# Two small buffers for normalised tokens, one reader for each bank, and a changed product order in a two-half transformer block

## The chip, the cores and the metric

The kernel runs on one core of a Trainium2 chip. The metric is the device time of one execution in microseconds (us). Engines: PE (TensorE, matmuls), DVE (VectorE), ACT (ScalarE), POOL (GpSimd) and SP (SyncE, whose queue issues nearly all DMAs).

## The reference

```python
emb = silu(t) @ ada_w + ada_b                        # t: (2, 512), ada_w: (512, 3072)
shift_msa, scale_msa, gate_msa, shift_mlp, scale_mlp, gate_mlp = split(emb, 6)
norm = ln(x) * (1 + scale_msa) + shift_msa           # x: (2, 2048, 512)
h = gelu(norm @ ssm_w1 + ssm_b1)                     # 512 -> 512
x = x + gate_msa * (h @ ssm_w2 + ssm_b2)             # 512 -> 512
norm2 = ln(x) * (1 + scale_mlp) + shift_mlp
hf = gelu_tanh(norm2 @ ff_w1 + ff_b1)                # 512 -> 1024
out = x + gate_mlp * (hf @ ff_w2 + ff_b2)            # 1024 -> 512
```

All of it is in float32.

## The kernel before

The 4096 tokens are cut into 8 blocks of 512 (`NBLK`, `TB`); in memory a block is 128 partitions of C = 4 tokens. Every product is made by a scheme with seven smaller products, P1 to P7, in place of eight; its operands are quarters of a matrix and sums of quarters. `first` and `second` make the sums: s[0], s[1], s[2] and one changed quarter ("21" or "12"). P5 needs s[0], P6 s[1]. Of the weights, made by `first`, P7 is the changed "21" and P3 is s[2]; of the tokens, made by `second`, P3 is the raw quarter "22", P7 the changed "12" and P4 is s[2].

**The first half** goes by block. For each block `norm1(i)` loads x into one of five slots (`xs`, 8 KB a partition), takes the statistics on DVE, makes 1/sigma from them on POOL (`scales`), normalises the four tokens of a partition one by one on ACT (`normal`), and turns each on DVE (`turn`, 32x32 transposes) into one of two buffers (`blocks`). The turned block goes to `turned[i]` (two places of 8 KB, by the parity of i): for block 2 in 16 DMAs (`move`), for blocks 3 to 7 out to DRAM in four (`turned_out`) and in again in one. There ACT scales and shifts it in four steps (`modulate`), and `norm1_sums` makes the token sums. Then `ssm1(i)` makes the first product with gelu, `ssm2(i)` the second, added to x in its slot; the slot is written out (`x1_d`), and `norm2(i)` normalises and turns it for the second half, out to DRAM in four DMAs. In `norm1`, `normal` writes into `turned[i]`; in `norm2` it writes in place, into `xs[i]`.

Blocks 0 and 1 are turned by PE (`turn_rows_in`), and ACT or DVE scales and shifts them on the way out of PSUM (`turn_rows_out`). Block 0 goes in two halves of two tokens each: half 0 is turned between the two halves of the product that makes the scale (`modulation(1, 2)`), half 1 after it. For each half, rows k = 0, 1 share one PSUM bank and k = 2, 3 another; DVE takes even k, ACT odd.

PE's order is the order of the program: the block-0 head, `ssm1(0)`, `ssm2(0)`, two modulations, `ssm1(1)`, the gate rows, `ssm1(2)`, then for i = 1 to 7 `ssm2(i)`, `ssm1(i + 2)`. `ssm1(0)` takes its products in the order `FRESH`, the later ones in `CARRIED`; small pieces of PE work (`gate_rows_of(2, 1)`, the gate of `first_weight2`) stand between its products by `hooks`. Banks come in two sets that take turns by stage.

**The second half** takes pairs of blocks, four times `ff1(s)` and two `ff2`. Its weights (`weight_fw1`, `weight_fw2`) are prepared during the first half in the space of the modulation weights.

**Order on the other engines.** All work is recorded as operations (`Plan.add`) with estimated costs, and a planner (`Plan.order`) places them: it gives each operation the latest time at which it must be done for PE not to wait, simulates the engines, and writes the instructions out in the order of their planned starts. Each engine then runs its list in order. Dependencies are found by the cells that an operation reads and writes (`Plan.cells`; a PSUM bank is one cell). `plan.care` lengthens, for what is recorded while it is set, the planned latencies and DMA times; it is 0.15 for `norm1(2)`, and from `norm2(0)` to the end 0.3.

The tiles' names in the profile stand for regions: `turned` for both places of turned tokens, `ring`, `rows`, `far` and `fw` (`fw2_r`) for the regions with x slots, `hidden` and `near` for gelu's output and the second weights. In the blocks' sequence `fw` holds x of block 4, `rows` of 2, 3 and 7, `ring` of 1 and 6, `far` of 0 and 5. L292 is every matmul, L302 a transpose on PE, L254 every addition or multiplication of two tensors, L272 every activation, L281 every copy on ACT, L314 every DMA, L502 and L503 the statistics, L510 to L523 `scales`, L543 `turn`, L608 DVE's eviction of block 0's tokens.

Of the kernel before, what the change touches and what calls it, by code (L numbers as in the profile page):

```python
# [20 lines left out]
class Plan:  # L21
# [44 lines left out]
    def add(self, engs, fn, outs, ins, cost, lat, shared="", size=0, lead=0.0):  # L66
        op = Op()
        op.n, op.engs, op.fn, op.cost, op.lat, op.shared, op.size = len(self.ops), engs, fn, cost, lat, shared, size
        op.deps, op.succ, op.note, op.lead, op.care = set(), [], self.stage, lead, self.care
        op.after, op.done, op.sooner = None, None, 0.0  # L70
        for ap in ins:
            for c in self.cells(ap):
                if c in self.wrote:
                    op.deps.add(self.wrote[c])
                self.read.setdefault(c, []).append(op.n)
        for ap in outs:
            for c in self.cells(ap):
                if c in self.wrote:
                    op.deps.add(self.wrote[c])
                op.deps.update(self.read.pop(c, ()))  # L80
                self.wrote[c] = op.n
        op.deps.discard(op.n)
        self.ops.append(op)
        return op
# [112 lines left out]
def kernel(  # L197
# [20 lines left out]
    KD, KH = D // P, H // P  # L218
# [121 lines left out]
    def kb(t, at, n):  # L340
        return t[:, at * 256 : (at + n) * 256]

    def cut(t, form, **sizes):
        return t.rearrange(form, **sizes)
# [27 lines left out]
    w1_s = cut(kb(ring_r, 8, 6), "p (s k d) -> p s k d", s=3, k=2)  # L372
    w2_t = [cut(kb(near_r, at, 8), "p (k d) -> p k d", k=KD) for at in (0, 14)]
    w2_s = cut(kb(near_r, 8, 6), "p (s k d) -> p s k d", s=3, k=2)
    hA = [cut(kb(hidden_r, 8 * (i % 2), 8), "p (k t) -> p k t", k=KD) for i in range(NBLK)]
    hA_s = [cut(kb(hidden_r, 16 + 6 * (i % 2), 6), "p (s k t) -> p s k t", s=3, k=2) for i in range(NBLK)]
    blocks = [kb(far_r, 8 * n, 8) for n in range(2)]
# [88 lines left out]
    def gate_rows_of(g, bank):  # L466
        pa = rows_of(g, bank)
        tt("v", gate_rows[g], pa[:, :P], gate_b[g], ALU.add)
        to = gates_d[g].rearrange("b (n m q) -> m b n q", n=KD, q=G)
        for m in range(M):  # L470
            dma(to[m], cut(gate_rows[g][m * G : m * G + B, :], "p (n q) -> p n q", n=KD))
# [34 lines left out]
    def scales(t, mv, v="g", slots=slice(0, C)):  # L506
# [16 lines left out]
            small(v, lambda E: E.tensor_scalar(nmr, nmr, -1.0, None, ALU.mult), nmr, [nmr])  # L523
        return full[3], full[4]

    def normal(o, xt, c, rstd, nmr, e="a"):
        dst, src, b, s = o[:, c, :], xt[:, c, :], nmr[:, c : c + 1], rstd[:, c : c + 1]
        if e == "a":
            act(dst, src, AF.Identity, b, s)
        else:  # L530
            plan.add(
                "v",
                lambda E: E.tensor_scalar(dst, src, s, b, ALU.mult, ALU.add),
                [dst],
                [src, b, s],
                {"v": 560},
                {"v": 640},
            )

    def turn(bl, src, c):  # L540
        o = cut(bl, "p (m k c q) -> p k m c q", m=C, k=KD, c=C)[:, :, :, c, :]
        a = cut(src[:, c, :], "p (k m q) -> p k m q", k=KD, m=C)
        plan.add("v", lambda E: E.transpose(o, a), [o], [a], {"v": 636}, {"v": 705})  # L543

    def modulate(t, k, which, b):
# [5 lines left out]
    def next_blocks():  # L551
        turns[0] += 1
        return blocks[turns[0] % 2]
# [9 lines left out]
    def normed(src, dst, bl, queues="s"):  # L563
        t, mv = stats(src)
        rstd, nmr = scales(t, mv)
        for c in range(C):
            normal(dst, src, c, rstd, nmr)
            turn(bl, dst, c)
        return cut(bl, "p (m r) -> p m r", m=C)
# [7 lines left out]
    def turned_out(to, bl):  # L577
        for a in range(C):
            dma(to[:, a].rearrange("(m q) r -> q m r", m=C), bl[a * G : (a + 1) * G])

    def norm1(i):
        plan.stage = f"norm1 {i}"
        load_x(i)
        bl = normed(xs[i], turned[i], next_blocks())
        if i in turned1_d:
            turned_out(turned1_d[i], bl)
            dma(turned[i], turned1_d[i])
        else:
            move(turned[i], bl)
        for k in range(KD):  # L590
            modulate(turned[i], k, 0, i // PER_B)
        return norm1_sums(i)

    def turn_rows_in(xn, k, to, slots=range(C), ends=(True, True)):
        for c in slots:
            at = (c - slots[0]) * P
            turn_by_pe(to[:, at : at + P], xn[:, c, k * P : (k + 1) * P], ident, c == slots[0] and ends[0], c == slots[-1] and ends[1])

    def turn_rows_out(i, k, to, e, slots=range(C)):
        n = len(slots)  # L600
        o = turned[i][:, :, k * P : (k + 1) * P].rearrange("p a (c q) -> p a c q", c=C)[:, :, slots[0] : slots[0] + n]
        a = cut(to, "p (c a q) -> p a c q", c=n, a=C)
        shift, scale = mods[0][:, k, :1], mods[1][:, k, :1]
        if e == "v":
            cost = 128.0 * n / 0.96 + 70
            plan.add(
                "v",
                lambda E: E.tensor_scalar(o, a, scale, shift, ALU.mult, ALU.add),  # L608
                [o],
                [a, scale, shift],  # L610
                {"v": cost},
                {"v": cost + 90},
            )
        else:
            act(o, a, AF.Identity, shift, scale)
# [14 lines left out]

    def norm2(i):
        plan.stage = f"norm2 {i}"
        turned_out(turned_d[i], normed(xs[i], xs[i], next_blocks()))

# [18 lines left out]

    PLAIN = ("P1", "P2", "P6", "P5", "P7", "P3", "P4")

    FRESH = ("P1", "P2", "P5", "P6", "P7", "P3", "P4")

    def between(hooks, p, stage):  # L660
        if p in hooks:
# [450 lines left out]
        for c in (2 * h, 2 * h + 1):  # L1112
            normal(xn, xs[0], c, rstd, nmr, "va"[c % 2])

    def turn_in(h, bank, k0):
        for k in (k0, k0 + 1):
            turn_rows_in(xn, k, banks[bank][:, k % 2 * W : (k % 2 + 1) * W], range(2 * h, 2 * h + 2), (k == k0, k > k0))

    def turn_out(h, on):
        for k in range(KD):  # L1120
            to = banks[on[k // 2]][:, k % 2 * W : (k % 2 + 1) * W]
            turn_rows_out(0, k, to, "va"[k % 2], range(2 * h, 2 * h + 2))

    normed_half(0)
    plan.add("v", lambda E: E.tensor_copy(cols_t[:, :ROWS], banks[1][:, :ROWS]), [cols_t[:, :ROWS]], [banks[1][:, :ROWS]], {"v": 130}, {"v": 200})
# [10 lines left out]
    pick = cut(ident, "p (m q) -> p m q", q=G)[:, :, :1].to_broadcast([P, M, P])  # L1136
    plan.add("v", lambda E: E.tensor_copy(picks, pick), [picks], [ident], {"v": 560}, {"v": 640})
    modulation(0, 1)
    modulation(1, 2, lambda: (turn_in(0, 0, 0), turn_in(0, 3, 2)))
    turn_out(0, (0, 3))  # L1140
    normed_half(1)
    w1q = {"11": w1_t[:, :2, : D // 2], "12": w1_t[:, 2:, : D // 2], "21": w1_t[:, :2, D // 2 :], "22": w1_t[:, 2:, D // 2 :]}
    turn_in(1, 4, 0)
    turn_in(1, 6, 2)
    turn_out(1, (4, 6))
    w1_ops = first(w1q, thirds(w1_s), "g")
    tok = {0: norm1_sums(0)}
    load_gate_b(2)
# [15 lines left out]
        gated[0] = weight2(0, 2)  # L1164

    plan.anchor = len(plan.ops)
    hid = {0: ssm1(0, tok[0], w1_ops, {"P6": lambda: gate_rows_of(2, 1), "P3": first_weight2}, FRESH)}
    w2_ops = gated[0]
    load_ada(3)
    load_ada(4)  # L1170
    load_gate_b(5)
    plan.care = 0.15
    tok[2] = norm1(2)
    plan.care = 0.0
    ssm2(0, hid[0], w2_ops, PLAIN, {"P2": turn_first, "P5": turn_second})
# [3 lines left out]
    load_ada(5)  # L1179
    modulation(4, 2)  # L1180
    hid[1] = ssm1(1, tok[1], w1_ops)
    tok[3] = norm1(3)
    gate_rows_of(5, 1)
    hid[2] = ssm1(2, tok[2], w1_ops)
# [72 lines left out]
```

## Time and profile before

| | us |
|---|---|
| median of 3 runs | 575.43 |
| lowest and highest | 575.0 and 576.33 |
| the profiled execution | 576.46 |
| its span | 574.7 |
| busy: PE, DVE, POOL, ACT | 564.4, 460.9, 322.7, 240.6 |

The profile is of one execution; its times count from the start of the span. The TensorE clock was granted in full throughout. A float32 matmul leaves two records in the trace, so that a product of four matmuls is 8 records. At the end of a row, in brackets, stands how long the engine had been idle and who released it.

### The profile page before, as it was taken

The page shows a single profiled execution, that of the slowest core. Times are in us where ns is not written, and L with a number is a line of the kernel's source. Part 1 is how long each engine was busy: PE and PEld are TensorE (multiplying, and loading weights), DVE is VectorE, ACT ScalarE, POOL GpSimd, SP SyncE. Part 2 cuts the span into 40 slices and gives each one's busy share as a digit, 9 for nine tenths or more (in the row PEclk, how much of TensorE's full clock was granted, in tenths as well). Part 3 has the DMA queues.
Part 4 walks back from the last instruction along what each step waited for, and adds up shares of the span by engine and source line. Part 5 has one row for each costly group of instructions (what it writes and reads, how often), then busy time and mean ns, then how long its engine had stood idle before and what let it go on. Part 6 is the DMA issues. An engine that isn't in the chain of part 4 may idle for free.

```text
span 574.7 us, 9495 instructions
## 1 busy us (share of the span) xinstructions
PE 564.4 (98%) x3301; PEld 503.4 (88%) x3301; DVE 460.9 (80%) x875; ACT 240.6 (42%) x417; POOL 322.7 (56%) x410
## 2 busy tenths in 40 slices
PE   7999999999998999999999999999999999999997
PEld 4788888888887888888999888999888999888997
DVE  5587757769877888889886789888889996789846
ACT  3463955656585624656002366002265112335010
POOL 2794347989853689954800435802896643436620
PEclk9999999999999999999999999999999999999999
DMA  8953798889998976884225644137855053520022
GB/s 316 398 204 79 216 306 299 272 332 278 347 273 288 326 254 224 280 283 166 74 74 170 236 170 165 55 112 254 294 173 188 1 146 119 195 91 1 2 74 73
DMA packets 49659, 112.20 MB, mean 195 GB/s; under 512 B 5152, under 2 KB 9164, under 8 KB 48076
## 3 DMA queue, kind: packets, MB, share of 16 engines
q1 hardware_dynamic: 48848, 111.05, 58.1%
q8 instruction: 26, 0.43, 0.3%
q10 hardware_dynamic: 764, 0.55, 0.3%
q14 instruction: 21, 0.17, 0.1%
HBM read 73.69 MB, written 36.84 MB: 192 GB/s over the span
## 4 chain that ended last, share of the span: by engine, by line
PE 87%; DMA 6%; ACT 2%; DVE 1%; POOL 1%; issue 1%; SPq 1%; DVEq 0%; ACTq 0%; POOLq 0%
PE bank L292 87%; DMA turned<-turned 3%; DMA fw<-in_L_cond_ada_w_dram 1%; DMA ring<-in_x_dram 1%; ACT turned L272 1%; SPq L314 1%; ACT hidden L272 1%; ACT fw L272 0%; DVE hidden L254 0%; POOL ring L254 0%; DVE marks L502 0%; PE bank L302 0%; POOL near L254 0%; POOL turned L254 0%; DVE turned L608 0%
## 5 line engine op out<-in xcount | busy, mean ns | idle before, releaser
L292 PE MATMUL bank<-turned,ring 128*128 128x256 f32 x896 | 205.8, 380 | 3.2 <-ACT turned L272 1.7
L292 PEld LDWEIGHTS bank<-turned,ring 128*128 128x128 f32 x896 | 168.9, 190 | 29.0 <-ACT turned L272 2.9
L254 DVE TENSOR_TENSOR hidden<-bank,hidden 128x512 f32<-128x512 f32 (+2 forms) x171 | 125.8, 757 | 40.0 <-PE bank L292 34.4
L254 DVE TENSOR_TENSOR rows<-bank,rows 128x256 f32<-128x256 f32 (+3 forms) x234 | 99.2, 457 | 30.0 <-PE bank L292 23.4
L292 PE MATMUL bank<-near,hidden 128*128 128x256 f32 x448 | 98.4, 380 | 0.2 <-POOL near L254 0.2
L292 PEld LDWEIGHTS bank<-near,hidden 128*128 128x128 f32 x448 | 84.9, 190 | 12.1 <-POOL near L254 0.5
L292 PE MATMUL bank<-ring 128*128 128x256 f32 x336 | 82.2, 381 | 0.0
L292 PE MATMUL bank<-fw,hidden 128*128 128x128 f32 (+1 forms) x512 | 80.1, 301 | 0.0
L281 ACT COPY bank<-bank 128x512 f32<-128x512 f32 (+2 forms) x66 | 31.7, 480 | 109.5 <-PE bank L292 109.1
L292 PEld LDWEIGHTS bank<-fw,hidden 128*128 128x128 f32 x512 | 72.9, 191 | 3.9
L292 PEld LDWEIGHTS bank<-ring 128*128 128x128 f32 x336 | 63.2, 190 | 10.6 <-POOL hidden L254 1.1
L292 PE MATMUL bank<-fw,far 128*128 128x128 f32 (+2 forms) x624 | 66.0, 286 | 0.2 <-DMA fw<-in_L_cond_ada_w_dram 0.2
L254 POOL TENSOR_TENSOR fw<-fw 128x256 f32<-128x256 f32 (+1 forms) x59 | 53.2, 921 | 18.8 <-DMA fw_parts<-fw 8.4
L292 PEld LDWEIGHTS bank<-fw,far 128*128 128x128 f32 (+1 forms) x624 | 59.8, 166 | 3.2 <-issue 0.8
L292 PE MATMUL bank<-fw,near 128*128 128x128 f32 (+1 forms) x432 | 59.5, 291 | 0.0
L254 POOL TENSOR_TENSOR turned<-turned 128x512 f32<-128x512 f32 (+1 forms) x43 | 48.1, 1134 | 14.9 <-ACT turned L272 8.0
L272 ACT ACTIVATE hidden<-hidden,cols 128x512 f32<-128x512 f32 (+1 forms) x66 | 43.3, 707 | 31.0 <-DVE hidden L254 30.8
L292 PEld LDWEIGHTS bank<-fw,near 128*128 128x128 f32 x432 | 54.9, 192 | 1.4
L254 POOL TENSOR_TENSOR hidden<-hidden 128x512 f32<-128x512 f32 (+1 forms) x34 | 42.5, 1257 | 23.7 <-ACT hidden L272 16.2
L272 ACT ACTIVATE turned<-turned,mod,mod 128x512 f32<-128x512 f32 x56 | 41.9, 804 | 19.1 <-DMA turned<-turned 18.7
L254 POOL TENSOR_TENSOR ring<-turned,ring 128x256 f32<-128x256 f32 x40 | 29.2, 735 | 26.4 <-PE bank L292 15.1
L254 POOL TENSOR_TENSOR ring<-turned 128x256 f32<-128x256 f32 x14 | 10.2, 726 | 47.0 <-PE bank L292 43.8
(104 smaller groups left out, 560.2 us busy)
## 6 DMA issues: line engine op xcount, KB each, us to landing
ring<-fw_parts SPq DMA_DIRECT2D x28, 512.0 KB, 6.0
turned<-far SPq DMA_DIRECT2D x52, 256.0 KB, 4.6
ring<-fw_parts SPq DMA_DIRECT2D x28, 384.0 KB, 3.0
turned<-turned SPq DMA_DIRECT2D x32, 256.0 KB, 4.8
rows<-x SPq DMA_DIRECT2D x32, 256.0 KB, 4.9
out_dram<-rows SPq DMA_DIRECT2D x29, 256.0 KB, 2.9
fw<-in_L_cond_ff_w_dram SPq DMA_DIRECT2D x12, 512.0 KB, 4.8
fw_parts<-fw SPq DMA_DIRECT2D x21, 256.0 KB, 3.3
```

What stands on the lines that cost most here:

```text
L254: lambda E: E.tensor_tensor(o, a, b, f),
L272: lambda E: E.activation(o, a, func, bias=bias, scale=scale),
L281: plan.add("a", lambda E: E.copy(o, a), [o], [a], {"a": cost}, {"a": cost + 60})
L292: lambda E: E.matmul(o, lhsT, rhs, start=start, stop=stop, skip_group_check=True, **kw),
L314: plan.add(q, lambda E: E.dma_start(out=o, in_=a), outs, ins, {q: plan.ISSUE}, {q: lat}, size=size, lead=lead)
```

## The change

- `passing`, two buffers of 2 KB a partition in space that was free (in `near` and `hidden`): `normal` writes tokens c = 0 and 2 into the first, 1 and 3 into the second, and `turn` reads them there; for `norm1(2)` to `norm1(7)` and `norm2(1)` to `norm2(7)`. For these blocks `turned[i]` and `xs[i]` are not written by `normal` any more.
- Block 0's turned tokens: each bank has one reader. Half 0: k = 0 in bank 3 and k = 2, 3 in bank 0 for DVE, k = 1 in bank 6 for ACT. Half 1: banks 1, 7 and 4, all for ACT. So DVE makes three evictions and ACT five, where each made four.
- `FRESH`: P3 moves ahead of P7. (P5 was third before.) The gate rows go behind P5, where they were behind P6; `first_weight2` goes behind P7, where it was behind P3 (the sixth product in either order).
- The planner orders readers of one PSUM bank on different engines one after the other, as dependencies of its own.
- `plan.care`: 0 in place of 0.15 for `norm1(2)`; 0.45 in place of 0.3 from `norm1(3)` on.

By the planner the order on DVE, ACT, POOL and SP changes in many places up to the second half; the instructions themselves stay nearly the same in number (DVE has 6 more, POOL 7 fewer, some sums having moved between them, ACT 1 more). PE's instructions are the same, in an order that differs in the head alone.

```diff
@@ Plan.add
+                if len(c) == 1:
+                    op.deps.update(n for n in self.read.get(c, ()) if self.ops[n].engs != engs)
...
+    passing = (kb(near_r, 24, 2), kb(hidden_r, 30, 2))
...
+    def slot(t, c):
+        return t[c % 2] if isinstance(t, tuple) else t[:, c, :]
@@ normal
-        dst, src, b, s = o[:, c, :], xt[:, c, :], nmr[:, c : c + 1], rstd[:, c : c + 1]
+        dst, src, b, s = slot(o, c), xt[:, c, :], nmr[:, c : c + 1], rstd[:, c : c + 1]
@@ turn
-        a = cut(src[:, c, :], "p (k m q) -> p k m q", k=KD, m=C)
+        a = cut(slot(src, c), "p (k m q) -> p k m q", k=KD, m=C)
@@ norm1
-        bl = normed(xs[i], turned[i], next_blocks())
+        bl = normed(xs[i], passing, next_blocks())
@@ norm2
-        turned_out(turned_d[i], normed(xs[i], xs[i], next_blocks()))
+        turned_out(turned_d[i], normed(xs[i], passing if i else xs[i], next_blocks()))
...
-    FRESH = ("P1", "P2", "P5", "P6", "P7", "P3", "P4")
+    FRESH = ("P1", "P2", "P5", "P6", "P3", "P7", "P4")
...
-    def turn_in(h, bank, k0):
-        for k in (k0, k0 + 1):
-            turn_rows_in(xn, k, banks[bank][:, k % 2 * W : (k % 2 + 1) * W], range(2 * h, 2 * h + 2), (k == k0, k > k0))
-
-    def turn_out(h, on):
+    ROOM = (((3, 0), (6, 0), (0, 0), (0, 1)), ((1, 0), (7, 0), (4, 0), (4, 1)))
+
+    def room(h, k):
+        bank, part = ROOM[h][k]
+        return banks[bank][:, part * W : (part + 1) * W]
+
+    def turn_in(h):
         for k in range(KD):
-            to = banks[on[k // 2]][:, k % 2 * W : (k % 2 + 1) * W]
-            turn_rows_out(0, k, to, "va"[k % 2], range(2 * h, 2 * h + 2))
+            turn_rows_in(xn, k, room(h, k), range(2 * h, 2 * h + 2), (k != 3, k != 2))
+
+    def turn_out(h):
+        for k in range(KD):
+            turn_rows_out(0, k, room(h, k), ("vavv", "aaaa")[h][k], range(2 * h, 2 * h + 2))
...
-    hid = {0: ssm1(0, tok[0], w1_ops, {"P6": lambda: gate_rows_of(2, 1), "P3": first_weight2}, FRESH)}
+    hid = {0: ssm1(0, tok[0], w1_ops, {"P5": lambda: gate_rows_of(2, 1), "P7": first_weight2}, FRESH)}
...
-    plan.care = 0.15
+    plan.care = 0.0
     tok[2] = norm1(2)
...
     hid[1] = ssm1(1, tok[1], w1_ops)
+    plan.care = 0.45
     tok[3] = norm1(3)
```

More of the change, by code (lines that the diff above doesn't have):

```diff
@@ L1138 @@
     modulation(0, 1)
-    modulation(1, 2, lambda: (turn_in(0, 0, 0), turn_in(0, 3, 2)))
-    turn_out(0, (0, 3))
+    modulation(1, 2, lambda: turn_in(0))
+    turn_out(0)
     normed_half(1)
     w1q = {"11": w1_t[:, :2, : D // 2], "12": w1_t[:, 2:, : D // 2], "21": w1_t[:, :2, D // 2 :], "22": w1_t[:, 2:, D // 2 :]}
-    turn_in(1, 4, 0)
-    turn_in(1, 6, 2)
-    turn_out(1, (4, 6))
+    turn_in(1)
+    turn_out(1)
     w1_ops = first(w1q, thirds(w1_s), "g")
```

## The prediction

> **What bounds the kernel now.** I read the parts of the page first, then busy time by stage, then TensorE's waits, then the timeline around each wait. The first part of the page shows one engine at the limit:
>
> ```profile
> PE 564.4 (98%) x3301; PEld 503.4 (88%) x3301; DVE 460.9 (80%) x875; ACT 240.6 (42%) x417; POOL 322.7 (56%) x410
> ```
>
> PE is busy for 564.4 of 574.7 us. The change alters neither the number nor the shape of any matmul; only in the head does it move some. So it can win only PE's idle time, and lose only by making more of it. Busy time by stage says where that is (after the length, each engine's busy us):
>
> ```profile
> 45.00:60.00 15.00, 15.00 (x135) 12.83 (x128) 9.85 (x26) 6.55 (x12) 4.89 (x16) 1.00 0.46 113
> ...
> 108.00:157.00 49.00, 48.62 (x226) 42.52 (x225) 37.83 (x76) 28.74 (x50) 45.06 (x66) 1.00 0.92 314
> 157.00:183.00 26.00, 24.28 (x113) 21.05 (x113) 21.80 (x41) 15.87 (x28) 11.17 (x19) 1.00 0.91 289
> ...
> 219.00:574.00 355.00, 351.54 (x2164) 322.23 (x2162) 296.02 (x550) 115.19 (x202) 175.86 (x185) 1.00 0.44 147
> ```
>
> From 219 on, the second half of the network, nearly all is PE: 351.54 of 355 us, and what is missing is mostly the last additions and the write. Between 45 and 60 PE never rests, between 108 and 157 it misses 0.38 us and between 157 and 183 1.72 us. TensorE's waits name the places:
>
> ```profile
> PE bank L292 <- ACT turned L272: 1.7, 1, 1.7
> ...
> PE bank L292 <- POOL turned L254: 0.9, 1, 0.9
> PE bank L292 <- DVE hidden L254: 0.4, 1, 0.4
> PE bank L292 <- POOL near L254: 0.2, 1, 0.2
> ```
>
> The 0.9 is in block 0's first product, the 0.4 in `ssm1(4)`, the 1.7 ahead of `ssm1(7)`; the 0.2 is in `ssm2(0)`. Little more than these can be won after the first 14 us, where nothing that the change touches binds.
>
> **The head (bank rooms, P3 ahead of P7).** The timeline of the head:
>
> ```profile
> 13.38 0.99 DVE L608 TENSOR_SCALAR turned<-bank,mod,mod 128x256 f32<-128x256 f32 x2
> ...
> 13.98 5.67 PE L292 MATMUL bank<-turned,ring 128*128 128x256 f32 x24 [0.21 <-DVE turned L608]
> 14.02 1.48 ACT L272 ACTIVATE turned<-bank,mod,mod 128x256 f32<-128x256 f32 x3 [2.01 <-DVE turned L608]
> ...
> 14.65 1.27 POOL L254 TENSOR_TENSOR ring<-ring 128x512 f32<-128x512 f32 x1 [4.57 <-DMA ring<-in_L_cond_ssm_w_dram]
> ...
> 16.10 0.56 ACT L272 ACTIVATE turned<-bank,mod,mod 128x256 f32<-128x256 f32 x1 [0.61 <-DVE turned L608]
> ...
> 16.70 0.69 DVE L254 TENSOR_TENSOR turned<-turned 128x512 f32<-128x512 f32 x1 [0.63 <-ACT turned L272]
> 17.23 0.33 SPq L314 DMA_DIRECT2D rows<-in_x_dram  x1
> 17.53 1.27 POOL L254 TENSOR_TENSOR ring<-ring 128x512 f32<-128x512 f32 x1 [1.61 <-DVE turned L254]
> ...
> 18.76 1.72 POOL L254 TENSOR_TENSOR turned<-turned 128x512 f32<-128x512 f32 x1
> ...
> 20.53 2.00 PE L292 MATMUL bank<-turned,ring 128*128 128x256 f32 x8 [0.88 <-POOL turned L254]
> ...
> 23.55 3.69 PE L292 MATMUL bank<-turned,ring 128*128 128x256 f32 x16
> ...
> 27.08 1.05 PE L292 MATMUL bank<-hidden,fw 128*128 128x128 f32 x8
> ```
>
> The eight evictions of block 0's turned tokens share banks between DVE and ACT, and each reader waits for the other (2.01 and 0.61 us on ACT), so the last ends at 16.66. Only then come DVE's sum s0 (16.70), POOL's weight sum behind it (17.53), POOL's token sum s1 (18.76, 1.72 long), and at 20.53 P6, which needs both. PE had finished P1, P2 and P5, 24 records from 13.98. Two products, 16 records, take 3.53 from the start at 23.55 to the next start at 27.08, 0.221 a record; 24 of these end at 19.28. So 20.53 - 19.28 = 1.25 us are lost.
>
> After the change the banks have one reader each, three evictions on DVE and five on ACT. An eviction takes 0.99 / 2 = 0.50, so from 13.38 DVE ends at 14.9 and ACT at 15.9. s0 needs only two early ones on ACT beside DVE's first: it can start at 14.95 and P5, at 17.5, has it. POOL's weight sum then follows its first one from about 15.9 on, and s1 ends near 18.5. The gate rows (formerly after P6; 23.55 - 20.53 less P6's 8 records is 1.25) now stand between P5 and P6, so P6 is due only at 20.5; their weights had landed by 17.2, when the row load that reuses that queue slot was issued. Cover for s1 is 2.0 us. The sum of q12 goes from DVE to POOL, and P3, which reads raw tokens, stands ahead of P7, which needs it: POOL's six sums in a row, at 1.27 each from 14.65, end at 22.3, and P7 is due at 20.5 + 2 x 1.77 = 24.0. The whole 1.25 goes: **-1.25**. Bounds: 0 if another sum is late by as much, and -1.4 if the waits inside P1 go too. I take -1.25 because each successor keeps over a microsecond of cover.
>
> [...]
>
> **Block 2's tokens (passing buffers, care 0).** With PE 1.25 earlier, what is due next? `ssm1(2)` at 59.39:
>
> ```profile
> 40.87 0.69 DVE L254 TENSOR_TENSOR far<-bank,far 128x512 f32<-128x512 f32 x1 [0.65 <-PE bank L292]
> ...
> 42.05 2.83 DVE L543 STREAM_TRANSPOSE far<-turned 128x512 f32<-128x512 f32 x4 [0.48 <-ACT turned L272]
> ```
>
> ```profile
> 44.95 10.94 SPq L314 DMA_DIRECT2D turned<-far  x16
> ...
> 46.26 1.26 DVE L502 BATCH_NORM_STATS2 marks<-rows 128x6 f32<-128x512 f32 x2
> ...
> 57.98 2.93 ACT L272 ACTIVATE turned<-turned,mod,mod 128x512 f32<-128x512 f32 x4 [0.35 <-issue]
> ...
> 59.39 2.86 PE L292 MATMUL bank<-turned,ring 128*128 128x256 f32 x12
> ```
>
> Four normalisations, four transposes, 16 moves on SP's queue (10.94), then ACT's four modulations from 57.98, 0.73 apart. P1 reads the first two; they end at about 58.8 and 59.5, for matmuls at 59.39 and 59.83. The margin is 0.3 to 0.6 us. The program's order of the changed kernel moves this chain back against PE: DVE's four transposes stand behind four statistics of block 3 and the addition that starts at 40.87. That addition is released by PE, so it comes at 39.6; with 0.69, two statistics (1.26 in the row at 46.26) and an aggregate the first transpose starts at about 41.7. The two small buffers now bind: normalisation 2 can start only when transpose 0 has ended (42.4), and so on through 0.8 and 0.7 us: transpose 3 ends at 44.6, against 42.05 + 2.83 = 44.88. The moves start only 0.3 earlier where PE comes 1.25 earlier. First matmul: ready 58.5, due 58.1, 0.4 lost; second: ready 59.2, due 58.9, 0.25 lost. **+0.65**. Bounds: 0, if the transposes come a microsecond sooner; +1.5, if block 3's tokens are awaited in front of them. The nearest rows are these.
>
> **Blocks 3 to 7 (passing buffers, care 0.45).** Two stalls remain:
>
> ```profile
> 95.76 12.25 PE L292 MATMUL bank<-near,hidden 128*128 128x256 f32 x56
> ...
> 107.84 10.52 PE L292 MATMUL bank<-turned,ring 128*128 128x256 f32 x48
> 107.95 0.41 SPq L314 DMA_DIRECT2D ring<-in_x_dram  x1
> ...
> 115.93 1.29 DVE L502 BATCH_NORM_STATS2 marks<-ring 128x6 f32<-128x512 f32 x2 [1.84 <-DMA ring<-in_x_dram]
> ...
> 117.93 0.67 DVE L254 TENSOR_TENSOR hidden<-bank,hidden 128x512 f32<-128x512 f32 x1
> ...
> 118.75 1.53 PE L292 MATMUL bank<-turned,ring 128*128 128x256 f32 x6 [0.39 <-DVE hidden L254]
> ```
>
> A product pair sequence of 56 records takes 107.84 - 95.76 = 12.08, 0.216 a record; 48 end at 118.19, and PE goes on at 118.75: 0.56 lost. DVE's addition at 117.93, which empties PE's bank, was behind statistics that waited for the load of x, issued at 107.95 and landed at 115.9. In the changed order all statistics of that time stand at the end of `ssm2(2)`'s additions, that is before 108, and x's slot is given back by ACT's normalisation and no longer by the in-place copy's transpose. The load is issued earlier on SP, right behind block 4's tokens. **-0.56**; bounds 0 and -0.56.
>
> ```profile
> 159.28 1.52 ACT L272 ACTIVATE turned<-rows,marks 128x512 f32<-128x512 f32 x2
> ...
> 162.16 6.62 SPq L314 DMA_DIRECT2D turned<-far  x8
> ...
> 168.89 3.88 SPq L314 DMA_DIRECT2D turned<-turned  x5
> 168.90 12.25 PE L292 MATMUL bank<-near,hidden 128*128 128x256 f32 x56
> ...
> 179.18 5.75 ACT L272 ACTIVATE turned<-turned,mod,mod 128x512 f32<-128x512 f32 x8 [7.78 <-DMA turned<-turned]
> ...
> 182.87 7.51 PE L292 MATMUL bank<-turned,ring 128*128 128x256 f32 x32 [1.72 <-ACT turned L272]
> ```
>
> ```profile
> 171.86 7.22 DMA turned<-turned
> ```
>
> `ssm1(7)` should follow 168.90 + 12.08 = 180.98 and starts at 182.87: 1.89 lost, to ACT's modulations, which waited for a load issued at 171.86. It took 7.22 us, behind four loads for the second half (the row at 168.89 holds all five). Block 7 was normalised at 159.28 into the place where it was to be loaded. In the changed order this load stands ahead of those four, two fw2 loads and one weight write before it, and ACT's modulations stand at the beginning of `ssm2(5)`, some 10 us before they are due. **-1.89**; bounds 0 (queue held by the fw2 loads, which wait for POOL) and -1.89.
>
> The new waits of the passing buffers lie on ACT: in each of 13 normalised blocks the third and fourth normalisation wait for a transpose, with ACT's next evictions queued behind them. Back to back two normalisations take 1.52 (159.28) and a transpose 0.7, so where DVE is prompt the wait is nothing. I put it at 0 where DVE is free; below nothing is excluded, since ACT does no less. The new dependencies between bank readers exist in the planner alone; they issue nothing.
>
> **Sum.** -1.25 + 0.65 - 0.56 - 1.89 = -3.05. The profiled execution took 576.46 (span 574.7), 1.03 above the median of 575.43; so changed, it would take 573.4, and the median 572.4.
>
> **Rivals.**
>
> Slower: ACT stuck behind the passing buffers. DVE is busy for 37.83 of the 49 us from 108 to 157, so a transpose can find one or two additions or statistics of 0.7 ahead of it; ACT stands meanwhile, and the copy of P1's sum behind it has only P5's 1.73 us of cover, less its own 0.57. Some eight of the 13 blocks have such a copy, or an eviction, close behind a waiting normalisation. It decides from 1.2 us of backlog on; 0.7 over at eight places is +5.6, and the time 575.43 - 3.05 + 5.6 = 578.0. Against it: the order is planned with these buffers, and most of the normalisations stand right behind a copy, not ahead. Chance 0.16.
>
> Block 7's load stays late: SP is one queue, in front of the load stand transfers that wait for POOL. Then -1.89 is missing: 574.3. For it: SP's issues of five loads took 3.88 us here. Against: 10 us of slack. Chance 0.15.
>
> POOL binds in the head. A DVE sum beside POOL's stretched it here to 1.72 from 1.27; if that happened four times and each cost a DVE sum's 0.7, POOL would be ready at 22.3 + 4 x 0.7 = 25.1 for P7 at 24.0, and 1.1 us would be lost: 573.5. [...] Chance 0.05.
>
> The change does not do what its title says: P5 stood third before already. What moves is P3 ahead of P7, which is worked out above; no separate time.
>
> **How the numbers follow.** The forecast has 0.64, the rivals 0.16, 0.15 and 0.05. The forecast's own range is 571.2 (no stall at block 2, all else gone: -3.7, and half a microsecond for the gap in `ssm2(0)`) to 573.9 (block 2 at +1.5 and the 0.56 kept). To hold 8 in 10 I go from 571.0 to 576.6, which takes in the late load and the start of the slower rival. About 0.2% (1.15 us) is what a measurement of this kernel can tell: faster lies below 574.3, slower above 576.6. The forecast and the head's rival are faster (0.69), of the late load about a third: 0.74; the rest of it is the same, 0.10; slower 0.16.
>
> **What would show it.** In the changed trace: P6 within 0.2 us of the end of the gate rows, no PE idle between 14 and 26; a wait of `ssm1(2)` for ACT's modulations of 0.4 to 0.7; none at `ssm1(4)` and `ssm1(7)`, with ACT's modulations of block 7 done by 175; PE's idle time between 14 and 219 below 1.5 us. I am wrong if ACT's evictions or seeds appear among PE's releasers with over a microsecond, or if the second half starts less than 1.5 us earlier than before.

## The result, and the profile after

| | before | changed |
|---|---|---|
| median of 6 runs, us | 575.97 | 573.32 |
| lowest and highest | 575.0 and 576.98 | 572.86 and 573.73 |
| the profiled execution | 576.46 | 572.99 |
| its span | 574.7 | 571.2 |

The ratio is 0.9953 with a 95% interval of 0.9939 to 0.9966: the changed kernel is faster by 2.65 us. The two profiled executions differ by 3.47. In the changed kernel's rows the lines have moved by 2 to 6: L294 is every matmul, L304 PE's transpose, L256 every addition of two tensors, L274 every activation, L316 every DMA, L505 the statistics, L549 `turn`, L614 DVE's eviction.

The first part of the page and busy time by stage (length, then the busy us of PE, PEld, DVE, ACT and POOL):

```profile
PE 564.3 (99%) x3301; PEld 504.1 (88%) x3301; DVE 466.2 (82%) x881; ACT 242.9 (43%) x418; POOL 314.0 (55%) x403
```

```profile
14.00:219.00 205.00, 204.88 (x1066) 179.18 (x1067) 163.56 (x317) 124.80 (x213) 145.46 (x219) 1.00 0.85 280
...
219.00:570.00 351.00, 347.47 (x2144) 318.48 (x2142) 294.65 (x539) 112.95 (x198) 165.18 (x171) 1.00 0.44 144
```

Before, the same stretch from 14 to 219 reads so:

```profile
14.00:219.00 205.00, 201.76 (x1046) 174.94 (x1047) 156.87 (x299) 120.67 (x209) 143.49 (x211) 1.00 0.82 272
```

PE's work is as it was (564.3 us, 3301 records). In the first half its idle time has gone from 3.24 to 0.12 us. TensorE's waits, the whole list:

```profile
PE bank L294 <- POOL half L321: 1.3, 1, 1.3
PE bank L294 <- DVE hidden L256: 0.6, 1, 0.6
PE bank L304 <- DMA fw<-in_L_cond_ssm_b_dram: 0.5, 1, 0.5
PE bank L294 <- DVE turned L614: 0.2, 1, 0.2
```

The first and third stand before the first product, the fourth at its start. The second is new, and the timeline shows it in the second half, in the third pair of blocks:

```profile
426.33 0.93 DVE L256 TENSOR_TENSOR fw<-fw 128x256 f32<-128x256 f32 x1 [0.42 <-POOL fw L256]
...
427.19 7.85 DVE L256 TENSOR_TENSOR hidden<-bank,hidden 128x1024 f32<-128x1024 f32 x9
...
429.60 1.03 PE L294 MATMUL bank<-turned,ring 128*128 128x256 f32 x4
...
431.20 1.99 PE L294 MATMUL bank<-turned,ring 128*128 128x256 f32 x8 [0.58 <-DVE hidden L256]
```

The planner has put one sum of the second weights (`fw<-fw`) on DVE ahead of the additions that empty PE's banks. That sum took 0.93 us beside a sum of POOL that ran until 426.98; one of the same size took 0.41 at 119.53, while POOL rested. The records at 431.20 start 1.60 after the four at 429.60, which take 0.86: 0.75 is lost. Before, DVE had no such sum there, and PE ran through.

The head, in the timeline of the changed kernel:

```profile
13.48 1.45 DVE L614 TENSOR_SCALAR turned<-bank,mod,mod 128x256 f32<-128x256 f32 x3
13.54 2.39 ACT L274 ACTIVATE turned<-bank,mod,mod 128x256 f32<-128x256 f32 x5 [1.15 <-DVE mod L467]
14.08 5.45 PE L294 MATMUL bank<-turned,ring 128*128 128x256 f32 x24 [0.21 <-DVE turned L614]
...
15.05 1.53 DVE L256 TENSOR_TENSOR turned<-turned 128x512 f32<-128x512 f32 x1
...
16.73 1.27 POOL L256 TENSOR_TENSOR ring<-ring 128x512 f32<-128x512 f32 x1 [0.69 <-DVE turned L256]
...
17.95 1.28 POOL L256 TENSOR_TENSOR turned<-turned 128x512 f32<-128x512 f32 x1
...
19.46 1.08 PE L294 MATMUL bank<-fw,far 128*32 128x128 f32 x32
...
20.47 5.45 PE L294 MATMUL bank<-turned,ring 128*128 128x256 f32 x24
21.65 2.51 POOL L256 TENSOR_TENSOR turned<-turned 128x512 f32<-128x512 f32 x2
...
25.75 1.05 PE L294 MATMUL bank<-hidden,fw 128*128 128x128 f32 x8
```

ACT's five evictions run in one piece, without the two waits for DVE. The 24 records of P1, P2 and P5 take 5.38 from 14.08 to the gate rows at 19.46, against 6.55 before (13.98 to 20.53), and the gate rows 1.01 against 1.25. The gate's matmul starts 11.67 after P1 and not 13.10: 1.43 less.

Block 2, and block 7:

```profile
43.64 0.71 DVE L549 STREAM_TRANSPOSE far<-hidden 128x512 f32<-128x512 f32 x1
...
44.49 10.57 SPq L316 DMA_DIRECT2D turned<-far  x16
...
56.84 2.94 ACT L274 ACTIVATE turned<-turned,mod,mod 128x512 f32<-128x512 f32 x4
...
58.01 2.21 PE L294 MATMUL bank<-turned,ring 128*128 128x256 f32 x9
```

```profile
164.28 1.94 SPq L316 DMA_DIRECT2D turned<-turned  x3
...
171.03 2.93 ACT L274 ACTIVATE turned<-turned,mod,mod 128x512 f32<-128x512 f32 x4 [1.63 <-DMA turned<-turned]
...
178.99 5.34 PE L294 MATMUL bank<-turned,ring 128*128 128x256 f32 x24
```

`ssm1(2)` at 58.01 waits for nothing, and block 7's modulations are done at 173.96, 5 us before the product at 178.99 that reads them.

Behind the head PE's records stand in the same order in both kernels, so their starts can be set against each other one by one. The first product starts 0.10 later; the head gains 1.43; a short wait behind the gate's matmul costs 0.14; `ssm2(0)` gains 0.19, `ssm1(4)` 0.62, the place ahead of `ssm1(7)` 2.32; the gap at 431 costs 0.83. The sum is -3.49, and the spans differ by 3.47. The wait ahead of `ssm1(7)` cost more than its own length: the kernel before had waited there for 1.72 us, the starts stood 1.88 further apart than the steady 0.216, and the next records lost another 0.44, of which 0.17 is a second wait, for ACT's second modulation.

### The profile page after: what moved, and what is told of

Its sections match the earlier page's. It is cut to its first block, busy times and chain, and to the rows that moved or that the text cites. A ratio compares the mean times of both kernels' runs of the same rounds, so it can differ in the third digit from the quotient of the medians.

```text
span 571.2 us, 9451 instructions
## 1 busy us (share of the span) xinstructions
PE 564.3 (99%) x3301; PEld 504.1 (88%) x3301; DVE 466.2 (82%) x881; ACT 242.9 (43%) x418; POOL 314.0 (55%) x403
## 4 chain that ended last, share of the span: by engine, by line
PE 97%; DMA 1%; DVE 1%; ACTq 0%; issue 0%; DVEq 0%
PE bank L294 96%; DMA fw<-in_L_cond_ssm_b_dram 1%; DVE hidden L256 1%; PE bank L304 1%; ACTq L316 0%; DVE rows L256 0%; DVE turned L614 0%; DVE bank L464 0%; DVE mod L467 0%; DVEq L256 0%
## 5 line engine op out<-in xcount | busy, mean ns | idle before, releaser
L294 PE MATMUL bank<-turned,ring 128*128 128x256 f32 x896 | 205.0, 380 | 0.8 <-DVE hidden L256 0.6
L294 PEld LDWEIGHTS bank<-turned,ring 128*128 128x128 f32 x896 | 169.2, 190 | 25.2 <-DVE hidden L256 1.4
L256 DVE TENSOR_TENSOR hidden<-bank,hidden 128x512 f32<-128x512 f32 (+2 forms) x171 | 125.2, 756 | 43.4 <-PE bank L294 39.4
L256 DVE TENSOR_TENSOR rows<-bank,rows 128x256 f32<-128x256 f32 (+3 forms) x234 | 99.3, 457 | 29.5 <-PE bank L294 22.0
L294 PE MATMUL bank<-near,hidden 128*128 128x256 f32 x448 | 98.3, 379 | 0.0
L294 PEld LDWEIGHTS bank<-near,hidden 128*128 128x128 f32 x448 | 85.0, 190 | 11.8 <-POOL near L256 0.3
L294 PE MATMUL bank<-ring 128*128 128x256 f32 x336 | 82.2, 381 | 0.1
L294 PE MATMUL bank<-fw,hidden 128*128 128x128 f32 (+1 forms) x512 | 80.1, 301 | 0.0
L294 PEld LDWEIGHTS bank<-fw,hidden 128*128 128x128 f32 x512 | 72.9, 191 | 3.9
L294 PEld LDWEIGHTS bank<-ring 128*128 128x128 f32 x336 | 63.2, 190 | 10.6 <-ACT bank L283 0.8
L294 PE MATMUL bank<-fw,far 128*128 128x128 f32 (+2 forms) x624 | 65.9, 286 | 0.0
L256 POOL TENSOR_TENSOR fw<-fw 128x256 f32<-128x256 f32 (+1 forms) x59 | 54.7, 945 | 17.7 <-DVE near L256 6.3
L294 PEld LDWEIGHTS bank<-fw,far 128*128 128x128 f32 (+1 forms) x624 | 59.8, 166 | 3.0 <-issue 1.2
L294 PE MATMUL bank<-fw,near 128*128 128x128 f32 (+1 forms) x432 | 59.5, 290 | 0.0
L256 POOL TENSOR_TENSOR turned<-turned 128x512 f32<-128x512 f32 (+1 forms) x44 | 49.4, 1139 | 16.6 <-ACT turned L274 6.4
L294 PEld LDWEIGHTS bank<-fw,near 128*128 128x128 f32 x432 | 54.9, 192 | 1.4
L274 ACT ACTIVATE hidden<-hidden,cols 128x512 f32<-128x512 f32 (+1 forms) x66 | 43.2, 707 | 29.2 <-DVE hidden L256 29.0
L256 POOL TENSOR_TENSOR hidden<-hidden 128x512 f32<-128x512 f32 (+1 forms) x31 | 37.9, 1224 | 26.7 <-ACT hidden L274 15.5
L274 ACT ACTIVATE turned<-turned,mod,mod 128x512 f32<-128x512 f32 x56 | 41.6, 803 | 8.7 <-DMA turned<-turned 4.5
L256 POOL TENSOR_TENSOR ring<-turned,ring 128x256 f32<-128x256 f32 x36 | 26.2, 731 | 25.6 <-PE bank L294 22.2
L256 POOL TENSOR_TENSOR ring<-turned 128x256 f32<-128x256 f32 x13 | 9.5, 728 | 50.2 <-PE bank L294 48.3
```

Of the source, the lines that this page charges most:

```text
L256: lambda E: E.tensor_tensor(o, a, b, f),
L274: lambda E: E.activation(o, a, func, bias=bias, scale=scale),
L294: lambda E: E.matmul(o, lhsT, rhs, start=start, stop=stop, skip_group_check=True, **kw),
```

## The experiments

Each stands beside runs of the kernel before on the same chip.

| run | median us | before | ratio, 95% interval |
|---|---|---|---|
| head edits only | 574.11 | 576.52 | 0.9957 (0.9944 to 0.9970) |
| passing buffers only | 574.13 | 576.52 | 0.9960 (0.9948 to 0.9972) |
| `care` only | 580.06 | 576.52 | 1.0058 (1.0043 to 1.0073) |
| changed, late weight sums on POOL | 572.17 | 576.52 | 0.9928 (0.9916 to 0.9940) |
| changed, `care` as before | 573.11 | 576.35 | 0.9949 (0.9935 to 0.9962) |
| changed, product order as before | 573.41 | 576.35 | 0.9950 (0.9938 to 0.9963) |
| changed, banks as before | 573.92 | 576.35 | 0.9960 (0.9948 to 0.9973) |
| changed, one passing buffer | 579.12 | 576.35 | 1.0057 (1.0044 to 1.0071) |
| `care` as before, late sums on POOL | 572.55 | 576.33 | 0.9934 (0.9910 to 0.9958) |
| the changed kernel again | 573.06 | 576.33 | 0.9941 (0.9920 to 0.9962) |

**Head edits only** (the changed kernel without `passing`, `care` as before):

```diff
-        bl = normed(xs[i], passing, next_blocks())
+        bl = normed(xs[i], turned[i], next_blocks())
...
-        turned_out(turned_d[i], normed(xs[i], passing if i else xs[i], next_blocks()))
+        turned_out(turned_d[i], normed(xs[i], xs[i], next_blocks()))
...
-    plan.care = 0.0
+    plan.care = 0.15
...
-    plan.care = 0.45
```

> The bank rooms and P3 ahead of P7 with the gate rows behind P5, without the passing buffers and with care 0.15 and 0.3 as before. Theory (each part removes its own stall): PE reaches the gate's first matmuls about 1.4 us earlier (27.08 to 25.7) and keeps that through ssm1(2); the stalls ahead of ssm1(7) (1.9 us) and in ssm1(4) (0.5) stay, since block 7 is still normalised into the place it is loaded to and its load stands among the four loads for the second half. Time -1.4 us, ratio 0.9976. Rival (what was won comes from the new order alone, whichever part causes it): the late stalls go here too, -3 us or more.

Measured: -2.4. The head is repaired in full: the gate's matmul starts at 25.65. But this is 1.0 more than the -1.4 that was expected. The gap in `ssm1(4)` is gone as well, without any passing buffer: given another head, the planner placed the statistics earlier, and they end by 113.5, where before two of them started at 115.93. And ahead of `ssm1(7)` there is about half of the former gap:

```profile
168.88 3.81 SPq L316 DMA_DIRECT2D turned<-turned  x5
...
179.09 2.93 ACT L274 ACTIVATE turned<-turned,mod,mod 128x512 f32<-128x512 f32 x4 [9.80 <-DMA turned<-turned]
...
179.95 2.27 PE L294 MATMUL bank<-turned,ring 128*128 128x256 f32 x8 [0.91 <-ACT turned L274]
```

The five loads still stand on SP together, ACT still waits 9.80 for the one it needs, and PE waits 0.91 (1.08 by its starts, against 1.88). What has moved is the order among the five: block 7's load, the one of 1024 KB among four of 256 KB, is issued third, at 171.43, where before it came last, at 172.46, and ACT takes its modulations first. So the late gaps belong to the order, not to the buffers alone. The head edits also bring a gap of 0.45 at 432.

**Passing buffers only** (before, with `passing`, `slot` and the two calls; old banks, product order and `care`, and without the planner's new dependencies):

```diff
+    passing = (kb(near_r, 24, 2), kb(hidden_r, 30, 2))
...
-        bl = normed(xs[i], turned[i], next_blocks())
+        bl = normed(xs[i], passing, next_blocks())
...
-        turned_out(turned_d[i], normed(xs[i], xs[i], next_blocks()))
+        turned_out(turned_d[i], normed(xs[i], passing if i else xs[i], next_blocks()))
```

> The passing buffers alone; head, product order and care as before. Theory: the head keeps its idle 0.9 us, the gate's first matmuls start at 27.1; block 7's load stands ahead of the four loads for the second half, no wait ahead of ssm1(7); the statistics that stood before the addition in ssm1(4) stand before ssm2(2)'s end, no wait there. Time -2.4 us, ratio 0.9958. Rival (ACT held by the two-deep buffers): ACT's evictions and copies turn up among PE's releasers and eat half a microsecond or more of it.

Measured: -2.4. TensorE's waits:

```profile
PE bank L302 <- DMA fw<-in_L_cond_ssm_b_dram: 1.7, 1, 1.7
...
PE bank L292 <- POOL turned L254: 0.9, 1, 0.9
PE bank L292 <- DVE hidden L254: 0.4, 1, 0.4
PE bank L292 <- POOL near L254: 0.2, 1, 0.2
```

The 0.9 in the head and the 0.2 in `ssm2(0)` stay. The 1.7 for ACT ahead of `ssm1(7)` is gone, and so is the gap in `ssm1(4)`: the 0.4 here is at 434.5, in the second half. No activation of ACT holds PE up. Ahead of `ssm1(7)` it went as expected: block 7's load is the first of the five, issued at 166.55. So the buffers by themselves, too, remove both late gaps, and they bring one of 0.4.

**`care` only** (the kernel before, with two settings):

```diff
-    plan.care = 0.15
+    plan.care = 0.0
     tok[2] = norm1(2)
...
+    plan.care = 0.45
     tok[3] = norm1(3)
```

> The planner's care alone (0 for norm1(2), 0.45 from norm1(3) on), everything else as before. Theory: the load of block 7 still stands behind the four loads for the second half, and the normalisation still writes into its place: the wait ahead of ssm1(7) stays over 1 us, the head's idle time stays. Time within 0.7 us of before, either way. Rival (care is what counts): -2 us or more.

Measured: +3.5, where neither theory had it. Its waits and the timeline ahead of `ssm1(7)`:

```profile
PE bank L292 <- ACT turned L272: 4.0, 2, 3.3
```

```profile
171.41 2.74 SPq L314 DMA_DIRECT2D turned<-turned  x4
...
174.88 0.32 SPq L314 DMA_DIRECT2D turned<-turned  x1
...
184.06 2.93 ACT L272 ACTIVATE turned<-turned,mod,mod 128x512 f32<-128x512 f32 x4
...
184.92 4.29 PE L292 MATMUL bank<-turned,ring 128*128 128x256 f32 x10 [3.27 <-ACT turned L272]
```

One of the two waits (0.69) is ahead of `ssm1(2)`. It has the size of the loss that I had forecast there for the changed kernel, but not its path: without any small buffer the 16 moves start at 47.48, against 44.95 before. The other has grown to 3.27. Block 7's load is issued at 174.88, 2.4 us later than before (172.46), and ACT makes four modulations for the second half and three copies, from 179.68 to 184.06, ahead of block 7's; which of the two held it up is not separated. Behind this wait the matmuls themselves are slow, at a granted clock of 0.50, as the last section shows. By the starts `ssm1(2)` costs 1.04, the wait ahead of `ssm1(7)` 1.55 more than before, the slow matmuls 1.53, and `ssm1(4)` gains 0.62: +3.50, as the spans say (578.2 and 574.7).

**The changed kernel with late weight sums on POOL.** For the second batch of blocks, the sums of the `fw2` weights may not go to DVE:

```diff
-    def fw2_operands(make):
-        first_level = lambda q, s, **kw: second(q, s, **kw) if make else second_names(q, s)
+    def fw2_operands(make, e="vg"):
+        first_level = lambda q, s, **kw: second(q, s, e, **kw) if make else second_names(q, s)
...
-        return fw2_operands(True)
+        return fw2_operands(True, "vg" if bank else "g")
```

> The changed kernel with one thing more: the sums of the second batch's fw2 weights go on POOL only (the other engines' lists are the same up to there, PE's and SP's throughout). Theory: the new 0.75 us stall at 431 in the third pair of the second half comes from one such sum that the planner put on DVE between two evictions (0.93 us at 426.3, ahead of the addition that starts at 427.19); without it PE does not wait there, and the time is 0.7 us below the changed kernel, 572.6. Rival (that stall comes from DVE's additions themselves, or is a chance of one execution): the same time as the changed kernel, 573.3, with the wait still there or gone in both.

Measured: 572.17, the best of all. At the place of the new gap:

```profile
426.27 7.10 DVE L256 TENSOR_TENSOR hidden<-bank,hidden 128x1024 f32<-128x1024 f32 x8 [0.43 <-PE bank L294]
...
429.53 2.79 PE L294 MATMUL bank<-turned,ring 128*128 128x256 f32 x12
```

DVE starts its additions 0.92 sooner, as soon as PE's bank is ready, and PE's 12 records run through. With the sum on POOL, the wait is gone, and so is the 0.75: that is the cause, shown. The other traces of kernels with the head edits agree. Six have one such sum on DVE in the ten microseconds before this place (the changed kernel twice, head edits only, `care`, product order or banks as before), and they lose 0.45 to 0.86 by the starts; three have none (the sums on POOL twice, one passing buffer), and they lose nothing there.

**The changed kernel with `care` as before:**

```diff
-    plan.care = 0.0
+    plan.care = 0.15
     tok[2] = norm1(2)
...
-    plan.care = 0.45
     tok[3] = norm1(3)
```

> The changed kernel with care back at 0.15 and 0.3: head and passing buffers stay. Theory (the head and the buffers win, care only places the rest): no wait of PE between 14 and 219 over 0.3 us, the stall of the second half's third pair moves or goes with the order; time 572.0 to 573.3. Rival (the higher care is what keeps the late loads early enough, as the buffers alone leave them late): a wait of over 1 us ahead of ssm1(7) comes back, 574.5 or more.

Measured: 573.11. From 14 to 219 no gap is over 0.2; the only one behind is 0.46 at 430.2. With buffers and head in place, the two settings are worth nothing that can be measured.

**The changed kernel with the product order as before**, P7 ahead of P3, the gate rows behind P6:

```diff
-    FRESH = ("P1", "P2", "P5", "P6", "P3", "P7", "P4")
+    FRESH = ("P1", "P2", "P5", "P6", "P7", "P3", "P4")
...
-    hid = {0: ssm1(0, tok[0], w1_ops, {"P5": lambda: gate_rows_of(2, 1), "P7": first_weight2}, FRESH)}
+    hid = {0: ssm1(0, tok[0], w1_ops, {"P6": lambda: gate_rows_of(2, 1), "P3": first_weight2}, FRESH)}
```

> The changed kernel with P7 ahead of P3 and the gate rows behind P6, as before; the bank rooms stay. Theory (the rooms alone bring s1 early enough): POOL's s1 ends near 19.2, P6 is due at about 19.5, so PE waits 0.2 us at most in the head; its gate matmuls start at 25.6 to 25.9. Time within 0.4 us of the changed kernel. Rival (the gate rows as cover make the gain): a wait of 0.7 us or more ahead of P6.

Measured: 573.41. The head:

```profile
14.03 7.21 PE L294 MATMUL bank<-turned,ring 128*128 128x256 f32 x32 [0.21 <-DVE turned L614]
...
17.90 1.28 POOL L256 TENSOR_TENSOR turned<-turned 128x512 f32<-128x512 f32 x1
...
25.78 1.05 PE L294 MATMUL bank<-hidden,fw 128*128 128x128 f32 x8
```

P1, P2, P5 and P6 run as 32 records in one piece: s1 ends at 19.18, just in time. The bank rooms alone repair the head. By the starts, `ssm2(0)` and `ssm1(2)` are 0.2 and 0.4 worse than in the changed kernel, and the 0.14 behind the gate's matmul is absent.

**The changed kernel with the banks as before**, two readers for each bank:

```diff
-    ROOM = (((3, 0), (6, 0), (0, 0), (0, 1)), ((1, 0), (7, 0), (4, 0), (4, 1)))
+    ROOM = (((0, 0), (0, 1), (3, 0), (3, 1)), ((4, 0), (4, 1), (6, 0), (6, 1)))
...
-            turn_rows_in(xn, k, room(h, k), range(2 * h, 2 * h + 2), (k != 3, k != 2))
+            turn_rows_in(xn, k, room(h, k), range(2 * h, 2 * h + 2), (k % 2 == 0, k % 2 == 1))
...
-            turn_rows_out(0, k, room(h, k), ("vavv", "aaaa")[h][k], range(2 * h, 2 * h + 2))
+            turn_rows_out(0, k, room(h, k), ("vava", "vava")[h][k], range(2 * h, 2 * h + 2))
```

> The changed kernel with the old banks and readers (two rows a bank, DVE and ACT in turn); P3 ahead of P7 and the gate rows behind P5 stay. Theory (either edit of the head is enough): s1 ends at 20.5 as before, P6 is due at 20.5, POOL's four further sums end near 25 for P7 due at 24: PE waits 0.3 to 1.0 us in all, at P6 or P7. Time 573.5 to 574.3. Rival (the rooms make the gain): the whole 1.25 us comes back, in one wait ahead of P6, 574.6.

Measured: 573.92. P6 comes without a wait here too, behind the gate rows, and the gate's matmul starts at 25.88. What the old banks cost stands elsewhere, in TensorE's waits:

```profile
PE bank L294 <- POOL near L256: 0.6, 1, 0.6
PE bank L294 <- DVE hidden L256: 0.6, 1, 0.6
PE bank L294 <- ACT turned L274: 0.3, 1, 0.3
```

The 0.6 for POOL is in `ssm2(0)`, the 0.3 for ACT ahead of `ssm1(2)`. So for P6 either head edit is enough by itself. With the old banks block 2's modulations start at 58.16, with the new ones at 56.84: what the banks are worth beyond P6 is that the chains behind the head come sooner.

**The changed kernel with one passing buffer** in place of two:

```diff
-    passing = (kb(near_r, 24, 2), kb(hidden_r, 30, 2))
+    passing = (kb(near_r, 24, 2), kb(near_r, 24, 2))
```

> The changed kernel with one 2 KB buffer in place of two: each normalisation waits for the transpose before it. Theory (the buffers' depth binds only block 2, where the margin is 0.4 us): its four tokens take about 3 us longer, and PE waits 1.5 to 2.5 us ahead of ssm1(2); later blocks have cover. Time 574.8 to 576. Rival (ACT held behind transposes binds everywhere): waits of PE for ACT in most blocks of the first half, 578 or more. Second rival (slack everywhere, the planner moves the chain forward): under 0.5 us lost.

Measured: 579.12, 5.8 above the changed kernel. TensorE's largest wait and the timeline of block 3:

```profile
PE bank L294 <- ACT turned L274: 4.1, 2, 3.0
```

```profile
72.95 0.81 ACT L274 ACTIVATE near<-fw,marks 128x512 f32<-128x512 f32 x1
...
81.46 0.70 DVE L549 STREAM_TRANSPOSE far<-near 128x512 f32<-128x512 f32 x1
82.26 0.81 ACT L274 ACTIVATE near<-fw,marks 128x512 f32<-128x512 f32 x1 [7.20 <-DVE far L549]
...
86.43 2.91 ACT L274 ACTIVATE turned<-turned,mod,mod 128x512 f32<-128x512 f32 x4
...
87.28 3.02 PE L294 MATMUL bank<-turned,ring 128*128 128x256 f32 x10 [3.01 <-ACT turned L274]
```

ACT normalises a token of block 4 at 72.95, makes two other steps and then stands still for 7.20 us, until DVE gets to the transpose that empties the buffer; block 3's modulations are queued behind the remaining normalisations, and PE waits for 3.01. The other wait, 1.05, is at `ssm1(2)`. It is two places, neither block 2 alone nor every block. By the starts these two cost 3.9 and 1.4; gaps ahead of 41.33 and 222.69 cost 0.5 and 0.9, and the gap at 431 is absent, -0.8: 5.9, against 5.8 between the spans. What caused the two smaller gaps was not tested.

**`care` as before and late sums on POOL; the changed kernel again.** The first joins two edits that are shown above, the second is the changed kernel unaltered:

> The changed kernel with care back at 0.15 and 0.3, and the second batch's fw2 sums on POOL only. Theory (the second half's stall is one DVE sum ahead of an eviction; care moves nothing that PE waits for while the two buffers and the head's edits are there): no stall at 431, none over 0.3 us between 14 and 219; the same as the variant with the new care and these sums on POOL, 572.2, within 0.4. Rival (the new care is worth something by itself): 0.5 us or more above that.

> The changed kernel itself, again, beside the variant with old care and the fw2 sums on POOL. Theory: 573.3 as before, 0.7 to 1.0 above that variant, with the stall of the second half's third pair again in the trace, 0.6 to 0.8 us at the same place. Rival (the stall was a chance of one execution): no such stall, and the same time as the variant.

Measured: 572.55 and 573.06, beside each other. The gap at 431 is there again in the second (0.86) and absent in the first, so it is no chance of one execution. `care` as before adds nothing to what the weight sums bring (572.55 against 572.17, intervals overlapping). In both versions with the sums on POOL no wait of PE over 0.2 us is left between the start of the first product and the last one.

## Why the prediction was right

The forecast was 572.4 from a sum of -3.05; measured are 573.32 in the median and -3.47 between the profiled executions. Of the 0.92 between the medians 0.54 is the base, which has its median at 575.97 over six runs. The terms:

| step | forecast | measured |
|---|---|---|
| start of the first product | none | +0.10 |
| head | -1.25 | -1.43 |
| behind the gate's matmul | not foreseen | +0.14 |
| `ssm2(0)` | only in the range | -0.19 |
| block 2's tokens | +0.65 | 0 |
| `ssm1(4)` | -0.56 | -0.62 |
| ahead of `ssm1(7)` | -1.89 | -2.32 |
| addition behind a weight sum, at 431 | not foreseen | +0.83 |

*Head.* Right in mechanism and size. s0 started at 15.05 (forecast 14.95) but took 1.53, not 0.69, beside a sum of POOL that ran from 14.76 to 16.03; s0 ended 0.55 after it. PE lost nothing by it: s0 was there at 16.58 for P5 at 17.6, and s1 at 19.23 for P6 at 20.47. With the product order as before s0 took 1.54, beside a sum of POOL from 14.71 to 15.98; with the banks as before it took 0.69, and POOL had no sum between 15.93 and 17.54. The extra 0.2 of the head is the gate rows, which take 1.01 in their new place in place of 1.25; 0.14 of it is lost again behind the gate's matmul. What the prediction did not see is that it named two covers for one loss: the runs with one head edit taken back show that each alone suffices for P6.

*Block 2.* This step failed in its size: each link that I took for the chain was a little too late, and the last one most: 58.5 for the first modulation's end means a start at 57.7. The transposes ended at 44.35 (forecast 44.6), the 16 moves took 10.57, and ACT had no normalisation in front of the modulations, which began at 56.84 (before, one of 0.81 stood there at 56.81). The first, of 0.73, was ready at 57.6 for PE at 58.01. The margin of 0.4 is real but thin: with the old banks PE waits 0.31 there, and with one buffer 1.05.

*`ssm1(4)` and `ssm1(7)`.* Right in place, and a little too small in size, since only the waits were counted and not the slower records behind them. Block 7's load did go ahead of the four for the second half (164.28, the first of the row's three), and its modulations were done at 173.96, before the 175 that was named. One reading was wrong: the load issued at 171.86 in the kernel before is the last quarter, 256 KB, of a block of the second half. Block 7's own, 1024 KB, is the next, at 172.46, and the first four of ACT's eight modulations at 179.18 belong to the second half's block; block 7's begin at 182.02. So ACT's order had a part in that wait, beside the late load. The cause was also drawn too narrowly. I put both gaps to the passing buffers and `care`; the head edits by themselves removed the first and 0.8 of the second, and `care` is worth nothing that can be measured beside them. So the parts do not add: head alone -2.4, buffers alone -2.4, both together -2.65 to -3.3 in the three comparisons of this kernel or its twin with old `care`.

*The new gap.* It lies in the stretch of which the prediction said that nothing the change touches binds. It looked at the list of instructions up to the second half alone. Two errors of like size, +0.65 that did not come and +0.83 that was not foreseen, nearly cancel in the sum; that the sum came so close is in part luck. The upper end of the forecast's own range comes to 573.8 by its terms (575.43 - 1.25 + 1.5 - 1.89), not 573.9.

*Rivals.* "ACT stuck behind the passing buffers" did not happen: no ACT row is among PE's releasers. But it is no fancy; one buffer instead of two produces it, at one place with 7.20 us of ACT's time. Block 7's load did come early, and POOL's sixth sum in the head, which P7 reads, ended at 22.9 (21.65 and half of 2.51), with P7 due at 24.0: 0.6 later than in the sum of the prediction, and early enough. The rival in which POOL binds there reckons with 0.7 more for each of four sums of POOL, which no run here shows: before, one of POOL's sums in the head took 1.72 for 1.27, and in the changed kernel the six took 1.25 to 1.28 each.

The planner's new dependencies between bank readers order nothing here: the changed kernel's program has the same instruction lists with and without them. No run tests them alone.

## What to carry to other kernels

Where one engine is busy for 98% of the span, list its few waits with their places and price only those; a change then is worth what waits it removes, less what new ones the reordering makes, and both are of the same size. Edits to a planned program do not add: each redraws the whole order, so look for the new wait in the stretch that the edit does not touch (here a weight sum 400 us behind the head, put right by naming its engine). Two small buffers took the normalisations off the large tiles without a wait, while one tied ACT to DVE's backlog for 7 us.

## What the runs showed of the hardware

The run with `care` alone lost more than its wait. Busy time in stretches, the first of them the 3.27 us of idle PE (after POOL's busy time stand the granted clock, the DMA share and GB/s):

```profile
181.66:184.92 3.26, 0.00 (x0) 0.00 (x0) 3.23 (x8) 3.26 (x7) 0.00 (x0) 1.00 1.02 376
184.92:185.47 0.55, 0.55 (x2) 0.30 (x2) 0.55 (x2) 0.55 (x1) 0.00 (x0) 1.00 1.02 361
185.47:188.89 3.42, 3.42 (x9) 2.63 (x9) 3.02 (x6) 1.76 (x4) 1.27 (x1) 0.50 0.92 341
188.89:195.00 6.11, 6.11 (x30) 5.39 (x29) 3.83 (x8) 2.85 (x7) 5.69 (x8) 1.00 0.74 285
```

The granted clock falls to 0.50 at 185.47, when PE has been at work again for 0.55 us, and is back at 1.00 from 188.89. Ten steps from one record's start to the next, from 184.92 on, take 4.12 where the steady ones take 2.16; behind the wait of 1.72 in the kernel before, the same ten took 2.60. So the stretch at 0.50 cost 1.5 us beside the wait. Behind the wait of 1.72 before and that of 3.01 in the run with one buffer the clock stayed at 1.00 in the profiled executions (183 to 186, and 87 to 90). The lower clock here is one occurrence, behind a wait of 3.27 (3.43 by the starts of the records), and lasted 3.42; whether another wait of that length would be followed by the same, no run here shows.

The start varies from trace to trace: in the run with the passing buffers alone PE waited 1.7 us for a small load, against 1.1 in the kernel before and 0.5 in the changed one, and its first product began at 14.71 and not at 13.98 or 14.08. That is as much as most single steps here are worth, so such steps are to be read in the trace, not in one time.
